# Four layers on one core: masks ahead, layer 0's mix in source order on VectorE and ScalarE, first norm row by row, a scaling halfway, statistics spread

## The chip, the cores and the metric

The kernel runs on one core of a Trainium2 chip, in one launch, with all data in F32. The metric is the device time in microseconds (us). The engines are TensorE (PE; its weight loads are listed apart as PEld), VectorE (DVE), ScalarE (ACT), GpSimd (POOL) and SyncE (SP), whose queue issues most of the DMAs. Each engine works through its own instructions one after the other.

## The reference

The input is 8 images of 56 × 56 positions with 192 channels. Four layers follow, each x + f(groupnorm(x)) with 32 groups:

```python
x = x + L0(_gn(x))   # p,q,v = silu(x@w+b); qv = q*v; out = (p*(toeplitz along w + toeplitz along h of qv)) @ o_w + o_b
x = x + L1(_gn(x))   # layer norm; rolled 7x7 windows, 6 heads, bias and mask added to the scores, softmax; projection
x = x + L2(_gn(x))   # 192 -> 384; 3x3 depthwise conv; mix of four exponential scans; layer norm; 384 -> 192
x = x + L3(_gn(x))   # 7x7 depthwise conv; layer norm; 192 -> 768, gelu, 768 -> 192; times gamma
return x
```

A group norm needs the mean and the variance of a whole image, so that each image's scale and shift come after its last element of the layer before. The layer norms are over the channels of one position.

## The kernel before, in words

**Stages.** The program goes layer by layer, each layer over all 8 images, with DRAM scratch between the steps. Image tiles have 128 partitions: 64 channels for the upper half of the image and the same 64 for the lower, by 3 channel groups j. Layer 0 has a first step (`layer0_qv`, L358, q and v of all images, written to the DRAM arrays left and right) and a second (`layer0_mix`, L463). Layer 1 takes four rows of windows per image. Layer 2 is `layer2_in` (L811), `layer2_mix` (L845, by channel groups over all images) and a loop over `layer2_out` (L968). Layer 3 begins with `layer3_in` (L983), which is interleaved with layer 2's output, then a depthwise convolution and the two large products.

**Order.** An instruction outside a `tc.manual_schedule(engines=...)` gets its place on its engine from a planner, which at compile time lists the instructions by the times it expects. Within such a block the engines named keep the order of the source; the others are still planned. Before the change layer 1's loop has PE in source order (L1279), the loop with layer 2's output and layer 3's input has VectorE (L1341), and the end of layer 3 has PE, ScalarE and VectorE (L1406). Layer 0 has none. `tc.keep_in_program_order` (in `layer2_in`) fixes single instructions. Tiles have a number of buffers (`bufs`, the pool's number where none is given): a write to a tile waits until the readers of the buffer's last use have ended, and a read waits for the write or the DMA.

**Masks.** `build_bias_mask` (L301) prepares attention bias plus mask for layer 1, in eight parts, during `layer0_qv` of images 1 on. `eighth(g)` (L324) clears the tile mk, which has one buffer, on GpSimd, loads two halves into it, adds six heads' bias on VectorE (L331) into bmt, one buffer as well, and stores bmt to DRAM (L334). q and v of the layer (L371 products, L377 bias addition on VectorE, L378 silu on ScalarE) run beside it.

**Mix.** For each image there are three passes g over channel chunks. A pass takes steps of 8 channels: `right_operand` copies part of a block's tile rt into rc (L409, on VectorE in even steps and ScalarE in odd ones, three buffers), `left_operand` copies lt into lc on GpSimd (two buffers), 8 or 16 small products go into one of two PSUM tiles op (L417), and the engine of that step copies op to o (L532). Operands are copied two steps ahead. A block's lt and rt are loaded by SyncE (L401), with two buffers each; pass 0 and 1 have four blocks of four steps, pass 2 one of eight. Between the steps of a pass, `between` runs the steps of the gate of the pass before (`layer0_gate`, L419): products pj (L429), silu on ScalarE (L434), transposes of o into ot, their product on VectorE (L443), products y (L450), and the addition to x on VectorE (L458). At the end of pass 0 the group norm's scaling xn of the image is written by three VectorE instructions, and the next image's x is loaded.

**First norm of layer 1.** `layer1_norm` (L622) is a generator. For each of four rows it writes xr on ScalarE (L636), the mean as a product (L644), subtracts on VectorE (L646), squares on ScalarE (L648), the variance as a product (L652) and copies it to rs (L653). After the fourth row it takes one square root (L654) and one reciprocal (L655) of all rows, and then for each row spreads rs by a product (L660) and multiplies (L662). For image 0 all of it is run before the first scores' Q, V and E parts (Q is L679); for the others, its steps are taken where `plan` (L1278) has an N.

**Layer 2's input.** `layer2_in` scales the image's x to xn in three VectorE instructions (L818), clears the padding on GpSimd (L821), then runs 15 tiles of products (L830, four PSUM tiles), each added to the bias on VectorE into pt (L838), and stores pt.

**Layer 2's output and layer 3's input.** For each image there are four groups k of rows and three j. Each (k, j) gives a product (L975) and the addition to x (L980). Pieces of the next image's layer norm statistics (`ln_pieces`, L190) come at i = 3k + j from 3 to 8; the steps of the image before's `layer3_in` are taken in between. `layer3_in` begins with 12 `bn_stats` (L144), two of its yields among them, goes on to the group sums (gh_m, L168), then the scaled image zp, its transposes zps (L1015) and the store.

Of the kernel before, what the change touches and what calls it, by code (L numbers as in the profile page):

```python
# [77 lines left out]
def kernel(ctx: ExitStack, tc: tile.TileContext, a: dict, out: bass.AP):  # L78
# [222 lines left out]
    def build_bias_mask(psum, pool, masks):  # L301
# [22 lines left out]
        def eighth(g):  # L324
            mk = pool.tile([128, 4, WN], F32, name="mk", bufs=1)
            nc.gpsimd.memset(mk, 0.0)
            for r in range(2):
                nc.gpsimd.dma_start(mk[64 * r:64 * r + WN], mask[g, r])
            bm = pool.tile([128, 3, 4, 2, WN], F32, name="bmt", bufs=1)
            for h in range(HEADS):  # L330
                nc.vector.tensor_tensor(  # L331
                    bm[:, h % 3, :, h // 3, :], mk, bt[:, h:h + 1, :].to_broadcast([128, 4, WN]), ALU.add
                )
            nc.gpsimd.dma_start(bmask[g], bm.rearrange("p a b c d -> p (a b c d)"))  # L334

        masks += [lambda g=g: eighth(g) for g in range(8)]
# [285 lines left out]
    def layer1_norm(b, x, pool, psum, consts):  # L622
# [7 lines left out]
        rs = pool.tile([128, TT], F32, name="rs1")  # L630
        yield xr
        sc, sh = scsh1[:, b, 0], scsh1[:, b, 1]
        for g in range(4):
# [19 lines left out]
            nc.vector.tensor_copy(rs[32 * g:32 * g + 32], vp)  # L653
        nc.scalar.activation(rs, rs, AF.Sqrt, bias=eps5)  # L654
        nc.vector.reciprocal(rs, rs)  # L655
        for g in range(4):
            yield
            gs = bass.ts(g, TT)
            bp = psum.tile([128, 512], F32, name="rstd", tag="mm", bufs=3)[:, 0:TT]
            nc.tensor.matmul(bp, sel[32 * g:32 * g + 32], rs[32 * g:32 * g + 32], start=True, stop=True)  # L660
            xs = xw[:, :, gs]
            nc.vector.tensor_tensor(xs, xs, bp.unsqueeze(1).to_broadcast([128, 3, TT]), ALU.mult)  # L662
# [148 lines left out]
    def layer2_in(b, x, pool, psum, w_in, b_in):  # L811
# [10 lines left out]
        nc.gpsimd.memset(xn[64:128, :, R2 - 3:R2, 0:W], 0.0)  # L822
        pt = pool.tile([128, C2, P2], F32, name="pt")
        nh = R2 // 2
        for i in range(nh):
# [12 lines left out]
            nc.vector.tensor_tensor(dst, ps[:, 0:ns, 0:C2], b_in[:, v, 0:ns], ALU.add)  # L838

# [128 lines left out]
    def layer2_out(k, j, y, x, psum, w_out):  # L968
# [11 lines left out]
        nc.vector.scalar_tensor_tensor(xs, ps[:, 0:nt], vec("b_out", j), xs, ALU.add, ALU.add)  # L980


    def layer3_in(b, x, zp, pool, psum):  # L983
# [3 lines left out]
        st = pool.tile([128, 3, NTH, 6], F32, name="gh_st")  # L987
        mv = pool.tile([128, 1, 3, 2], F32, name="gh_mv")
        for t in range(NTH):
            gn_piece(st, x, t)  # L990
            if t % 2:
                yield
# [228 lines left out]
    with ExitStack() as st:  # L1221
# [19 lines left out]
        layer0_mix(pool, blocks, psum, ops, w_p, w_o, loaded)  # L1241


    with ExitStack() as st:
# [23 lines left out]
        for _ in steps:  # L1268
            pass
# [256 lines left out]
```

## Time and profile before

| what | us |
|---|---|
| three runs of the kernel | 6127.55 median (6127.48 to 6136.09) |
| the profiled execution | 6119.55 |
| its span, with a mean granted PE clock of 0.943 | 6117.8 |
| PE busy | 5451.9 (89%) |
| VectorE busy | 3401.5 (56%) |
| ScalarE busy | 2216.8 (36%) |
| GpSimd busy | 1330.2 (22%) |

The span goes from the first instruction to the last in the profiled execution; the rest of its own time, 1.75 us, lies around it. The stages by that execution's clock: layer 0's first step 0 to 872, its mix 872 to 2103, layer 1 to 3440, layer 2's input to 3757, layer 2's mix to 4392, layer 2's output with layer 3's input to 4913, the convolution to 5252, and layer 3's products to 6118.

In a row of the timeline the first number is the start, the second the duration; then come engine, line and operation, out<-in by the program's names, and in brackets the idle time before it with what ended it. Rows of like instructions are put together with their number (x6).

### The profile page before, as it was taken

How to read it: one execution, taken by the hardware profiler on the slowest of the kernel's cores; microseconds unless marked ns; L12 is line 12 of the kernel's file. 1: busy time of each engine (PE TensorE's matmuls, PEld its weight loads, DVE VectorE, ACT ScalarE, POOL GpSimd, SP SyncE). 2: the span in 40 equal slices, each digit the busy share in tenths (PEclk: the TensorE clock that was granted, in tenths of full speed). 3: DMA queues.
4: the chain of work that ended last, by engine and by line, in shares of the span. 5: the costliest groups of instructions: out<-in, count | busy, mean ns of one | idle time of the engine just before them, and what ended most of it. 6: DMA issues, size and time to landing. Idle time of an engine off the chain costs nothing. (4 is left out here: it accounts for less than half of the span.)

```text
span 6117.8 us, 126576 instructions
## 1 busy us (share of the span) xinstructions
PE 5451.9 (89%) x55636; PEld 3509.4 (57%) x55636; DVE 3401.5 (56%) x4760; ACT 2216.8 (36%) x2938; POOL 1330.2 (22%) x867
## 2 busy tenths in 40 slices
PE   6799989999999888888888687999889889799999
PEld 5576766666666545555555455677544489444444
DVE  5677765565555445455454475888787601433331
ACT  2344444444444333333332101555466610333333
POOL 2100015444445212222222101433201100110100
PEclk8899999999999888999998898999989999899999
DMA  6799986666666614544533475667667588321210
GB/s 163 185 214 215 194 224 260 251 258 257 253 255 259 124 33 65 66 61 65 61 50 53 119 227 192 228 231 236 196 166 223 171 319 326 118 88 58 84 48 24
DMA packets 1034540, 1013.11 MB, mean 166 GB/s; under 512 B 826136, under 2 KB 958196, under 8 KB 1007220
## 3 DMA queue, kind: packets, MB, share of 16 engines
q1 hardware_dynamic: 1019424, 940.93, 54.5%
q0 software_dynamic: 8416, 39.40, 2.0%
q10 hardware_dynamic: 6148, 24.68, 1.3%
q8 instruction: 437, 7.16, 0.5%
q14 instruction: 115, 0.94, 0.0%
HBM read 676.28 MB, written 345.08 MB: 167 GB/s over the span
## 5 line engine op out<-in xcount | busy, mean ns | idle before, releaser
L371 PE MATMUL qv<-w_qv_sb,xn 64*112 64x288 f32 x5376 | 724.6, 426 | 51.1 <-DVE act L377 47.8
L409 POOL COPY lc<-lt 128x896 f32<-128x896 f32 (+1 forms) x320 | 572.7, 1806 | 620.4 <-PE op L417 602.6
L371 PEld LDWEIGHTS qv<-w_qv_sb,xn 64*112 64x112 f32 x5376 | 532.7, 184 | 238.1 <-DVE act L377 64.4
L378 ACT ACTIVATE act<-act 112x576 f32<-112x576 f32 x448 | 300.3, 682 | 462.1 <-DVE act L377 424.4
L1154 PE MATMUL ph<-y,w_sb 64*128 64x392 f32 x2304 | 398.4, 498 | 6.4 <-ACT hid L1158 6.4
L1165 PE MATMUL po<-hid,w_sb 128*64 128x392 f32 x2304 | 386.3, 494 | 0.0
L429 PE MATMUL pj<-xn,w_p_sb 64*128 64x392 f32 (+1 forms) x1920 | 373.4, 515 | 13.8 <-issue 10.5
L417 PEld LDWEIGHTS op<-rc,lc 128*56 128x56 f32 x9216 | 308.1, 136 | 127.1 <-issue 66.1
L417 PE MATMUL op<-rc,lc 128*56 128x56 f32 x9216 | 339.4, 221 | 43.9 <-POOL lc L409 25.7
L450 PE MATMUL y<-pp,w_o_sb 128*64 128x392 f32 (+1 forms) x1920 | 356.2, 504 | 21.9 <-DVE x L458 12.7
L377 DVE TENSOR_TENSOR act<-qv,b_qv 112x576 f32<-112x576 f32 x448 | 320.8, 751 | 90.8 <-PE qv L371 90.4
L1172 DVE TENSOR_TENSOR x<-x,z 128x392 f32<-128x392 f32 x96 | 71.0, 740 | 522.1 <-ACT z L1170 522.1
L409 ACT COPY rc<-rt 128x896 f32<-128x896 f32 (+1 forms) x160 | 256.8, 1605 | 238.7 <-PE op L417 219.8
L881 PE MATMUL cv<-zc,wt 128*128 128x224 f32 x1536 | 312.8, 355 | 24.2 <-DMA zc<-pd 24.2
L881 PEld LDWEIGHTS cv<-zc,wt 128*128 128x128 f32 x1536 | 290.2, 189 | 67.8 <-issue 51.9
L443 DVE TENSOR_TENSOR pp<-pp,ot 128x784 f32<-128x784 f32 (+1 forms) x160 | 154.6, 966 | 313.2 <-ACT pp L434 293.7
L1154 PEld LDWEIGHTS ph<-y,w_sb 64*128 64x128 f32 x2304 | 220.3, 188 | 176.3 <-issue 26.2
L729 POOL TENSOR_TENSOR e<-e,mx 128x1176 f32<-128x1176 f32 x64 | 139.8, 2184 | 812.5 <-DVE mx L728 629.6
L1055 PE MATMUL cps<-zc,wt 128*128 128x224 f32 x1536 | 299.1, 355 | 16.7 <-DMA zc<-zd 15.6
L830 PE MATMUL pin<-w_in_sb,xn 64*128 64x384 f32 x1392 | 251.5, 511 | 60.4 <-POOL xn L821 60.4
L1055 PEld LDWEIGHTS cps<-zc,wt 128*128 128x128 f32 x1536 | 289.0, 189 | 26.9 <-issue 19.4
L679 PE MATMUL qk_ps<-xr,wg 64*96 64x392 f32 x1536 | 299.5, 511 | 0.3 <-ACT oa L780 0.3
(211 smaller groups left out, 9113.6 us busy)
## 6 DMA issues: line engine op xcount, KB each, us to landing
lt<-left SPq DMA_DIRECT2D x72, 1792.0 KB
rt<-right SPq DMA_DIRECT2D x72, 1792.0 KB
left<-qv SPq DMA_DIRECT2D x224, 252.0 KB
right<-qv SPq DMA_DIRECT2D x448, 126.0 KB
wt<-in_band_dram SPq DMA_DIRECT2D x23, 2048.0 KB
wt<-in_band_dram SPq DMA_DIRECT2D x11, 4096.0 KB
zc<-pd SPq DMA_DIRECT2D x187, 232.0 KB
pd<-pt SPq DMA_DIRECT2D x7, 5568.0 KB
```

The lines of the kernel that those rows point to most:

```text
L371: nc.tensor.matmul(ps[s][:, which, 0:D1 // 2], xn[64 * s:64 * s + 64, j, bass.ts(i, 2 * W)], w_qv[64 * s:64 * s + 64, j, which, ns], start ...
L377: nc.vector.tensor_tensor(act, ps[s][:, :, 0:D1 // 2], b_qv[:, :, ns], ALU.add)
L378: nc.scalar.activation(act, act, AF.Silu)
L409: copy(c[:, 0:nu], raw.rearrange("p (w u d) -> p u d w", u=nu, d=64 // nu)[:, :, d0:d0 + 8])
L417: nc.tensor.matmul(op[64 * u:64 * u + W, i, :], lc[:, u, i], rc[:, u, i], start=True, stop=True)
L429: nc.tensor.matmul(ps[0:M, s, 0:TT], w_p[64 * s:64 * s + 64, j, d0:d0 + M], xn[64 * s:64 * s + 64, j, ts], start=(j == 0), stop=(j == 2),)
L450: nc.tensor.matmul(y[64 * s:64 * s + 64], w_o[0:M, c, 64 * j:64 * j + 64], pp[0:M, s], start=(c == gated[0][0]), stop=(c == gated[-1][0]),)
L679: nc.tensor.matmul(ps[s], wg[64 * s:64 * s + 64, j, c0:c0 + HC], xw[64 * s:64 * s + 64, j, gs], start=(j == 0), stop=(j == 2),)
L881: nc.tensor.matmul(dst, wt[:, c4 + i, 128 * q:128 * q + 128], zc[:, :, c4 + i, q:q + NPAIR], start=(q == 0), stop=(q == 1),)
L1055: nc.tensor.matmul(dst.rearrange("p (b n) -> p b n", n=NPAIR), wt[:, c4 + i, q * OP:(q + 1) * OP], zc[:, :, c4 + i, q:q + NPAIR], start=(q ...
L1154: nc.tensor.matmul(ps[:, s, 0:TT], w0[64 * s:64 * s + 64, j, m * 128:(m + 1) * 128], y[64 * s:64 * s + 64, j, ts], start=(j == 0), stop=(j ...
L1165: nc.tensor.matmul(ps[64 * s:64 * s + 64], w1[:, m, 64 * j:64 * j + 64], hid[:, m, s], start=(m == 0), stop=(m == 5),)
```

## The change

It has five parts. *Masks*: `eighth` is split into `load` and `add`, mk gets the pool's two buffers, mask 0 is loaded when the generator ends, and mask g + 1 is issued ahead of the addition of mask g. *Mix*: the call of `layer0_mix` stands in a `tc.manual_schedule` for VectorE and ScalarE. *First norm*: with `first=True` each row gets its own square root, reciprocal and multiplication; four steps (row 0 with its multiplication) run before the first scores, and the others one per part of the scores and then in the N steps. *Halfway*: the scaling of image b + 1 is a function of its own, `layer2_scale`, called after tile 7 of the 15 of image b (i = 7, so after eight tiles); image 0's is ahead of the loop. *Statistics*: each (k, j) of layer 2's output takes its own `bn_stats` right after the addition, `layer3_in` loses its 12 and two yields, the layer norm pieces are spread over i = 1 to 8 instead of 3 to 8, and the steps go one at a time up to i = 5 instead of 4.

```diff
@@ -321,19 +321,26 @@
             nc.vector.tensor_copy(bt[64 * r:64 * r + WN].rearrange("p h m -> p (h m)"), bp)
         mask = a["mask"].rearrange("(g q r) n m -> g r n q m", q=4, r=2)
 
-        def eighth(g):
-            mk = pool.tile([128, 4, WN], F32, name="mk", bufs=1)
+        mks = []
+
+        def load(g):
+            mk = pool.tile([128, 4, WN], F32, name="mk")
             nc.gpsimd.memset(mk, 0.0)
             for r in range(2):
                 nc.gpsimd.dma_start(mk[64 * r:64 * r + WN], mask[g, r])
+            mks.append(mk)
+
+        def add(g):
             bm = pool.tile([128, 3, 4, 2, WN], F32, name="bmt", bufs=1)
             for h in range(HEADS):
                 nc.vector.tensor_tensor(
-                    bm[:, h % 3, :, h // 3, :], mk, bt[:, h:h + 1, :].to_broadcast([128, 4, WN]), ALU.add
+                    bm[:, h % 3, :, h // 3, :], mks[g], bt[:, h:h + 1, :].to_broadcast([128, 4, WN]), ALU.add
                 )
             nc.gpsimd.dma_start(bmask[g], bm.rearrange("p a b c d -> p (a b c d)"))
 
-        masks += [lambda g=g: eighth(g) for g in range(8)]
+
+        load(0)
+        masks += [lambda g=g: (load(g + 1) if g < 7 else None, add(g)) for g in range(8)]
 
 
     def layer0_load(b, pool):
@@ -619,7 +626,8 @@
         rolled(x1[b], x, False, queues)
         return x
 
-    def layer1_norm(b, x, pool, psum, consts):
+    def layer1_norm(b, x, pool, psum, consts, first=False):
+
 
 
         ones2, ones32, sel = consts[4:]
@@ -628,6 +636,14 @@
         nc.gpsimd.memset(xr[:, 3 * NH:], 0.0)
         xw = xr[:, 0:3 * NH].rearrange("p (j n) -> p j n", j=3)
         rs = pool.tile([128, TT], F32, name="rs1")
+
+        def scaled(g):
+            gs = bass.ts(g, TT)
+            bp = psum.tile([128, 512], F32, name="rstd", tag="mm", bufs=3)[:, 0:TT]
+            nc.tensor.matmul(bp, sel[32 * g:32 * g + 32], rs[32 * g:32 * g + 32], start=True, stop=True)
+            xs = xw[:, :, gs]
+            nc.vector.tensor_tensor(xs, xs, bp.unsqueeze(1).to_broadcast([128, 3, TT]), ALU.mult)
+
         yield xr
         sc, sh = scsh1[:, b, 0], scsh1[:, b, 1]
         for g in range(4):
@@ -650,16 +666,22 @@
             vp = psum.tile([128, 512], F32, name="vps", tag="mm", bufs=3)[32 * g:32 * g + 32, 0:TT]
             for j in range(3):
                 nc.tensor.matmul(vp, ones32, sq[:, j], start=(j == 0), stop=(j == 2))
-            nc.vector.tensor_copy(rs[32 * g:32 * g + 32], vp)
+            if not first:
+                nc.vector.tensor_copy(rs[32 * g:32 * g + 32], vp)
+                continue
+            rg = rs[32 * g:32 * g + 32]
+            nc.scalar.activation(rg, vp, AF.Sqrt, bias=eps5[32 * g:32 * g + 32])
+            nc.vector.reciprocal(rg, rg)
+            yield
+            scaled(g)
+            yield
+        if first:
+            return
         nc.scalar.activation(rs, rs, AF.Sqrt, bias=eps5)
         nc.vector.reciprocal(rs, rs)
         for g in range(4):
             yield
-            gs = bass.ts(g, TT)
-            bp = psum.tile([128, 512], F32, name="rstd", tag="mm", bufs=3)[:, 0:TT]
-            nc.tensor.matmul(bp, sel[32 * g:32 * g + 32], rs[32 * g:32 * g + 32], start=True, stop=True)
-            xs = xw[:, :, gs]
-            nc.vector.tensor_tensor(xs, xs, bp.unsqueeze(1).to_broadcast([128, 3, TT]), ALU.mult)
+            scaled(g)
 
     def layer1_scores(g, xr, pool, psum, S, es, consts):
 
@@ -808,7 +830,7 @@
         queue.dma_start(x[64:128, :, 0:R2 - 3], src[:, :, R2 - 1:H])
         return x
 
-    def layer2_in(b, x, pool, psum, w_in, b_in):
+    def layer2_scale(b, x, pool):
 
         sc, sh = scsh2[:, b, 0], scsh2[:, b, 1]
         xn = pool.tile([128, 3, R2, 64], F32, name="xn2")
@@ -820,6 +842,10 @@
             ))
         nc.gpsimd.memset(xn[0:64, :, 0, 0:W], 0.0)
         nc.gpsimd.memset(xn[64:128, :, R2 - 3:R2, 0:W], 0.0)
+        return xn
+
+    def layer2_in(b, xn, pool, psum, w_in, b_in, halfway):
+
         pt = pool.tile([128, C2, P2], F32, name="pt")
         nh = R2 // 2
         for i in range(nh):
@@ -836,6 +862,8 @@
             dims = [list(z) for z in pt.ap]
             dst = bass.AP(pt.tensor, pt.offset + i, [dims[0], [nh, ns], [P2, C2]])
             nc.vector.tensor_tensor(dst, ps[:, 0:ns, 0:C2], b_in[:, v, 0:ns], ALU.add)
+            if i == nh // 2:
+                halfway()
 
         n = CG2 if b + 1 == nimg else 0
         if n:
@@ -965,7 +993,8 @@
                 bias=vec("be2", m), scale=vec("g2", m),
             )
 
-    def layer2_out(k, j, y, x, psum, w_out):
+    def layer2_out(k, j, y, x, st, psum, w_out):
+
 
         n0 = 4 * k
         nt = 2 * W * min(4, PH - n0)
@@ -978,18 +1007,14 @@
                 )
         xs = x[:, j, 2 * W * n0:2 * W * n0 + nt]
         nc.vector.scalar_tensor_tensor(xs, ps[:, 0:nt], vec("b_out", j), xs, ALU.add, ALU.add)
-
-
-    def layer3_in(b, x, zp, pool, psum):
+        nc.vector.bn_stats(st[:, j, k], xs)
+
+
+    def layer3_in(b, x, st, zp, pool, psum):
 
         sc = pool.tile([128, 1, 3], F32, name="sc3")
         sh = pool.tile([128, 1, 3], F32, name="sh3")
-        st = pool.tile([128, 3, NTH, 6], F32, name="gh_st")
         mv = pool.tile([128, 1, 3, 2], F32, name="gh_mv")
-        for t in range(NTH):
-            gn_piece(st, x, t)
-            if t % 2:
-                yield
         gn_aggregate(st, mv[:, 0])
         finish = gn_finish(mv, sc, sh, pool, psum, "gn")
         next(finish)
@@ -1238,7 +1263,8 @@
                 xpool.tile([128, 3, H // 2, W], F32, name="x1")
             x.append(layer1_load(0, xpool, (nc.sync, nc.gpsimd)))
 
-        layer0_mix(pool, blocks, psum, ops, w_p, w_o, loaded)
+        with tc.manual_schedule(engines={mybir.EngineType.DVE, mybir.EngineType.Activation}):
+            layer0_mix(pool, blocks, psum, ops, w_p, w_o, loaded)
 
 
     with ExitStack() as st:
@@ -1263,15 +1289,16 @@
 
         consts = (*consts, ones2, ones32, sel)
         xpool = x.pop(0)
-        steps = layer1_norm(0, x[0], pool, psum, consts)
-        xr = [next(steps)]
-        for _ in steps:
-            pass
+        own = layer1_norm(0, x[0], pool, psum, consts, True)
+        xr = [next(own)]
+        for _ in range(4):
+            next(own)
         if nimg > 1:
             x.append(layer1_load(1, xpool))
         values, (Q, V, E) = layer1_scores(0, xr[0], pool, psum, S, es, consts)
         for part in Q + [E[0], V[0], E[1], V[1]]:
             part()
+            next(own)
 
 
 
@@ -1300,6 +1327,7 @@
                     parts.update(zip("QVE", of_next))
                 for kind in plan:
                     if kind == "N":
+                        next(own, None)
                         next(steps, None)
                     elif parts.get(kind):
                         parts[kind].pop(0)()
@@ -1320,10 +1348,16 @@
         x = [layer2_image(0, xpool, nc.scalar)]
         w_in = resident("w_in", nc.scalar, pool)
         b_in = resident("b_in", nc.scalar, pool)
+        xn = [layer2_scale(0, x[0], pool)]
         for b in range(nimg):
             if b + 1 < nimg:
                 x.append(layer2_image(b + 1, xpool, nc.sync))
-            layer2_in(b, x[b], pool, psum, w_in, b_in)
+
+            def halfway():
+                if b + 1 < nimg:
+                    xn.append(layer2_scale(b + 1, x[b + 1], pool))
+
+            layer2_in(b, xn[b], pool, psum, w_in, b_in, halfway)
             if b == nimg - 3:
                 run(gn_finish(mv2[:, last], scsh2[:, last, 0], scsh2[:, last, 1], pool, psum, "pin"))
     with ExitStack() as st:
@@ -1372,13 +1406,15 @@
                         rows[0] = ln_rows(*var_next, eps5, pool)
                     following = scaled(*after, j)
                 if n >= 0:
-                    layer2_out(k, j, y, x[b], psum, w_out)
+                    if k == j == 0:
+                        gst = pool.tile([128, 3, 4, 6], F32, name="gh_st")
+                    layer2_out(k, j, y, x[b], gst, psum, w_out)
                     i = 3 * k + j
-                    if b + 1 < nimg and 3 <= i < 9:
-                        ln_pieces(st_next, ml[b + 1], range(NPAIR * (i - 3) // 6, NPAIR * (i - 2) // 6))
+                    if b + 1 < nimg and 1 <= i < 9:
+                        ln_pieces(st_next, ml[b + 1], range(NPAIR * (i - 1) // 8, NPAIR * i // 8))
                     if b + 1 < nimg and i == 8:
                         var_next = ln_var(in_halves(st_next), C2, pool)
-                    for _ in range(1 if i < 5 else 2):
+                    for _ in range(1 if i < 6 else 2):
                         next(steps, None)
                 if after and j < 2:
                     layer2_turned(after[1], j, following, y_next, psum)
@@ -1386,7 +1422,7 @@
             if k == 3:
                 run(steps)
                 nc.sync.dma_start(xd[b], x[b])
-                steps = layer3_in(b, x[b], zp, pool, psum)
+                steps = layer3_in(b, x[b], gst, zp, pool, psum)
         run(steps)
 
 
```

## The prediction

> **What bounds the kernel now.** The span is 6117.8 us, and TensorE is busy in 89% of it, so a part of the change is worth what it takes from TensorE's idle or cold time, or adds to it. I read the page's busy shares first, then windows over the five stretches that the change touches, then TensorE's list of waits, and last the tiles and timelines of the waits in question.
>
> Windows (start:end, length, then busy of PE, weight load, DVE, ACT, POOL, the granted clock, DMA share, GB/s):
>
> ```profile
> 225.00:310.00 85.00, 58.31 (x308) 42.55 (x308) 48.33 (x118) 18.63 (x28) 17.02 (x29) 0.76 0.66 162
> 874.00:2094.00 1220.00, 1144.51 (x15280) 755.44 (x15282) 696.80 (x906) 486.31 (x481) 574.83 (x325) 0.97 0.67 246
> 2103.00:2190.00 87.00, 53.15 (x546) 29.59 (x548) 33.13 (x37) 20.93 (x28) 12.73 (x14) 0.76 0.65 99
> 3469.00:3757.00 288.00, 255.73 (x1420) 148.77 (x1420) 201.71 (x148) 0.26 (x1) 14.63 (x34) 0.92 0.61 197
> 4395.00:4913.00 518.00, 434.53 (x2408) 223.11 (x2408) 362.86 (x688) 321.17 (x467) 58.85 (x78) 0.91 0.66 191
> ```
>
> In order they are the masks, layer 0's mix, the start of layer 1, layer 2's input product, and layer 2's output with layer 3's input. PE idles 26.7 us at the masks (85.00 − 58.31) at a clock of 0.76, about 75 us in the whole mix, and 32 us in layer 2's input. So there is much to win in short stretches, and little in the long one. What PE waited for:
>
> ```profile
> PE pin L830 <- POOL xn L821: 60.4, 8, 30.2
> PE tp L962 <- DVE yt L951: 57.9, 16, 16.9
> PE qv L371 <- DVE act L377: 47.8, 19, 6.0
> PE op L417 <- POOL lc L409: 25.7, 38, 1.9
> ```
>
> The first row is one start of 30.2 us and seven waits of (60.4 − 30.2)/7 = 4.3 us, one per image. About half of the third is the masks. The mask tile mk, and who waited for it:
>
> ```profile
>   DMA mk<-in_mask_dram: 34.6, 7
>   DVE bmt L331: 34.6, 7
> DMA to landing us min/median/max: 2.5/5.3/9.2
> ```
>
> VectorE stands 34.6 us before loads only just issued, and the bias additions of q and v (L377) are queued behind.
>
> **What the Trainium skill says.** "TensorE: Matmul & The Clock Gate", section "Part 1: The HAM clock gate", has PE fall to half clock after an idle window of a few us. The trace agrees: after a gap of 4.33 us the first tile of layer 2's input takes 3.70 us (start 3505.71, next eviction 3509.41) against 1.93 steady. The same page, "Architectural detail", says that ACT and DVE queues are strict FIFO: in the trace a Square stands ready at 2117.6 (VectorE's subtraction ends) and starts at 2126.58, behind activations that wait for a load. "ScalarE: Activation LUTs", "What ACT_TABLE_LOAD costs", gives 1283 ns; the trace shows 1.28 us at L654. "SBUF — State Buffer", "SBUF: two separate sides", says that VectorE and GpSimd share a port under a lock: a copy of rc (L409) takes VectorE 0.94 us alone and 2.15 beside GpSimd's copy of lc.
>
> **A, masks ahead.** A second mk buffer lets load g+1 start one image stretch before add g. The 34.6 us go. Late next is the bmt buffer, still single: the first addition waits for the store of the mask before, which lands 3.1 to 5.4 us after issue (median 4.2), with 0.8 to 2.2 us of other VectorE work between. About 3 us × 7 stay on VectorE, with the next L377 queued behind; PE's queued products hide 2 of each. PE keeps 7 × 1, and 4 of slow clock: −26 + 7 + 4 = **−15** (0, if the store is as late as the load was, to −26). GpSimd issues the same memset and DMAs, earlier.
>
> **B, mix in source order.** Nothing is added; the order of some 900 VectorE and 480 ScalarE instructions is fixed. The trace shows how far the present order is from it: 336 of 909 VectorE and 234 of 480 ScalarE instructions stand at their place in the source, most others within four places; what moves is that each rc copy comes one ahead of the gate's silu. Pass g = 1 (52.53 busy of 55 us) and g = 2 (47.00 of 47) are full of PE work, with two op buffers and three rc, so a silu or gate product in front of a copy costs about 0: what stands behind it on its engine, an rc or o copy, is needed two products later, and without that slack a pass would pay the 0.9 us of the silu per gate step. Pass g = 0 is different: its window shows DMA at 0.88, since a block's lt and rt take 4.7 us each and a block is used up in 9.5. ScalarE and SyncE there:
>
> ```profile
> 1505.36 0.53 ACT L532 COPY o<-op 120x448 f32<-120x448 f32 x1 [2.15 <-PE op L417]
> 1506.76 1.75 ACT L409 COPY rc<-rt 128x896 f32<-128x896 f32 x1 [0.87 <-PE op L417]
> 1508.84 0.91 ACT L434 ACTIVATE pp<-pj,vecs_sb 64x784 f32<-64x784 f32 x1 [0.33 <-PE pj L429]
> 1508.54 0.51 SPq L401 DMA_DIRECT2D rt<-right  x1
> ```
>
> The copy at 1506.76 is the last reader of its rt block; when it ends (1508.51) the next rt load goes out. In source order the silu is ahead of it, so the copy ends at 1508.84 + 0.91 + 1.75 = 11.5, 3.0 us later. If lt is loaded in that gap, most of it is covered; I take 0.65 us per block × 4 blocks × 8 images = +21, between 0 and 3.0 × 32 = 96. The three scalings to xn (5.2 us) now stand in one piece before the next rc and o: PE has 2 to 3 us to cover them, waits some 4 instead of 3: +8. The first pass and the last gate: +6 ± 6, with one gain against, since the wait of 10.5 us for x in the first pass (L429) falls to later, when x has long landed: −5. In all **+30** (−10 to +118).
>
> **C, first norm row by row.** Rows and PE at the start of layer 1:
>
> ```profile
> 2112.06 4.14 PE L644 MATMUL mean<-xr,ones 128*128 128x392 f32 x6
> 2127.84 4.10 PE L652 MATMUL vps<-sq,ones 128*32 128x392 f32 x6 [11.64 <-issue]
> 2162.45 5.89 PE L679 MATMUL qk_ps<-xr,wg 64*96 64x392 f32 x16
> ```
>
> Q starts 50 us after the first mean, when four rows are through. Row 0 alone from its vps at 2127.84: 2.2 products, 0.6 Sqrt and 1.28 table, 2.6 reciprocal, 1.7 rstd, 1.4 multiply: Q at about 2138, 24 us earlier, and up to 10 more if the Square isn't kept behind the waiting activations. Middle −28. Given back: rows 1 and 2 come between Q, E, V and the first softmax, 5 us of PE each, of which a softmax wait of 4.5 hides one: +5; row 3 in the N steps, with three more reciprocals of 2.6 on VectorE and table loads of 1.28, in front of copies that PE waits for: +5. **−18** (−3 to −30).
>
> **D, scaling halfway.** The turn of an image:
>
> ```profile
> 3501.42 0.84 DVE L838 TENSOR_TENSOR pt<-pin,b_in_sb 128x384 f32<-128x384 f32 x1 [0.39 <-PE pin L830]
> 3502.11 3.26 DVE L818 TENSOR_SCALAR xn<-x,scsh 128x1680 f32<-128x1680 f32 x3
> 3509.41 1.54 DVE L838 TENSOR_TENSOR pt<-pin,b_in_sb 128x768 f32<-128x768 f32 x1 [4.05 <-issue]
> ```
>
> The scaling is between two images with PE empty. Moved to tile 8 of 15, it has 15 × 1.93 = 29.0 us of products to hide in; VectorE's load per image is 14 × 1.54 + 0.84 + 3.3 = 25.7, and four PSUM tiles (7.7 us) carry PE over it. What is late next is x: its load takes 11.5 us and lands 6 us before halfway; with the store of pt (12 us) DMA has 23.5 of 29 us. New stage: 31.6 + 7 × 29.0 + 4.5 (the aggregate after image 5) = 239 against 287: **−48** (−30 to −52). Without the cover each image pays 3.3 us again, −25.
>
> **E, statistics spread.**
>
> ```profile
> 4879.23 5.70 DVE L144 BATCH_NORM_STATS2 gh_st<-x2o 128x6 f32<-128x392 f32 x12
> 4885.16 3.15 PE L168 MATMUL gh_m<-gh_mv,gmath_sb 128*128 128x1 f32 x14 [6.34 <-DVE gh_mv L148]
> ```
>
> The last image's 12 statistics stand bare before gh_m (6.34 us, and 3.15 cold against 1.72): −7. In the seven others they go from one place on VectorE to twelve, of equal sum; PE idles 6.5 us per period of 58.4, of which I take 1 each: −7. Against it, the first pieces at i = 1 want the next ml some 1 to 5 us before it lands (VectorE in order, so x2o waits behind): +4. **−10** (−25 to +10).
>
> **Sum.** −15 + 30 − 18 − 48 − 10 = −61. The profiled execution took 6119.55 us (span 6117.8 and 1.75 around it), so 6058.5; it lies 8 us under the median of 6127.55, and from that 6066.5 comes. I say **6065**.
>
> **Rivals.** (1) *Slower: the rt load behind the silu.* If the 3.0 us delay of L401 are all exposed, the 32 blocks of pass g = 0 cost 96 and B 96 + 22 (scalings 12, first pass 6, finish 4) = +118; with −91 for the rest, **6154**. It decides from (91 − 22)/32 = 2.2 us per block. For it: DMA runs at 0.88 there and the load is on its path. Against: lt is free to go first, and GpSimd already waits 0.64 for it. (2) *Source order is free*, B = 0: −91, **6036**. For it: PE idles only 75 us in the mix. (3) *New waits take the place of the old*: the bmt store gives A = 0, the row's Square stays behind the loads so that C = −5, D = −40, E = 0, B = +30: −15, **6112**. For it: single bmt buffer, load just in time. (4) *The planner's order differs so little that nothing shows*, within 0.2% (12 us, about what a measurement can tell): against it D, a plain removal.
>
> **Chances.** Forecast 0.37, rival 2 0.22, rival 3 0.14 (on the faster side), no change 0.05, rival 1 0.22: faster 0.73, same 0.05, slower 0.22. The low end is −91 with bounds of −30 more: 6005; the high end cuts through rival 1 at 6150.
>
> **What would show it.** mk's wait on VectorE from 34.6 to under 5, and one for the store instead; "pin <- POOL xn" from 60.4 to about 30; Q from 2162 (counted from the mix's end) 18 to 34 us earlier; gh_m's 6.34 under 2; the mix at 1250 instead of 1220, with rt issues of pass g = 0 at 10.2 instead of 9.5 apart. I am wrong if the mix grows by over 90, or layer 2's input doesn't fall under 250.

## The result and the profile after

The changed kernel takes 6107.52 us (median of 12 runs, 6095.21 to 6125.61), the kernel before 6128.76 (12 runs, 6110.45 to 6143.45): a ratio of 0.9967, with a 95% interval of 0.9954 to 0.9979. It is some 20 us faster, where 63 were forecast (6127.55 less 6065). The profiled execution took 6100.29 us, span 6098.5, 19.3 under the span before.

To see where the 19.3 us come from I took the start of the same products in both traces (the first of a stage or of an image) and subtracted:

| stretch | before | after | difference | forecast |
|---|---|---|---|---|
| start to the end of q and v (masks) | 869.4 | 850.8 | −18.6 | −15 |
| to the last y of the mix | 1232.4 | 1248.0 | +15.7 | +30 |
| to the first projection of layer 1's image 1 (first norm) | 290.2 | 279.8 | −10.5 | −18 |
| rest of layer 1, to the start of layer 2's input | 1077.8 | 1077.6 | −0.1 | 0 |
| layer 2's input (halfway) | 286.9 | 242.8 | −44.2 | −48 |
| layer 2's mix (not changed) | 633.2 | 637.5 | +4.3 | 0 |
| layer 2's output, layer 3's input (statistics) | 532.2 | 564.3 | **+32.1** | **−10** |
| rest | 1195.7 | 1197.7 | +2.0 | 0 |

The windows over the five stretches of the changed kernel, in the order and with the columns of the prediction's:

```profile
225.00:310.00 85.00, 67.10 (x438) 45.36 (x438) 59.20 (x137) 24.50 (x37) 15.24 (x26) 0.89 0.80 192
855.40:2091.10 1235.70, 1153.09 (x15286) 770.36 (x15287) 639.10 (x907) 471.42 (x481) 582.38 (x325) 0.97 0.65 243
2100.10:2187.10 87.00, 63.12 (x687) 35.05 (x689) 39.13 (x40) 31.21 (x43) 14.91 (x15) 0.74 0.64 97
3455.40:3699.60 244.20, 241.88 (x1420) 170.09 (x1420) 196.79 (x148) 0.27 (x1) 14.96 (x35) 0.97 0.72 232
4341.60:4891.70 550.10, 462.31 (x2408) 232.25 (x2408) 370.18 (x688) 321.94 (x467) 54.09 (x78) 0.88 0.62 180
```

Layer 2's input is now full: PE idles 2.3 of 244.2 us. In the last stretch the same 2408 products take 462 us of PE instead of 435, at a clock of 0.88 instead of 0.91. Most of the loss is here. PE's list of waits for the whole changed kernel:

```profile
PE tp L990 <- DVE yt L979: 65.6, 27, 18.5
PE op L424 <- DVE o L539: 32.2, 9, 16.3
PE pin L856 <- POOL xn L843: 30.1, 1, 30.1
```

The seven waits of 4.3 us of pin are gone and its start is left; the mix has got nine waits for o, of which one is of 16.3 us. VectorE's masks (waits of bmt):

```profile
DVE bmt L336 <- DMA bmask<-bmt: 16.9, 6, 5.0
```

As forecast, the load's 34.6 us are replaced by a shorter wait for the store of the mask before. The turn of an image in layer 2's input, on VectorE:

```profile
3486.93 0.86 DVE L864 TENSOR_TENSOR pt<-pin,b_in_sb 128x384 f32<-128x384 f32 x1 [0.39 <-PE pin L856]
3488.94 1.55 DVE L864 TENSOR_TENSOR pt<-pin,b_in_sb 128x768 f32<-128x768 f32 x1 [1.15 <-PE pin L856]
```

The next image's first eviction starts 2.0 us after the last of this one instead of 8.0, and no scaling stands between. PE at the start of layer 1:

```profile
2109.11 4.29 PE L660 MATMUL mean<-xr,ones 128*128 128x392 f32 x6
...
2132.76 7.34 PE L701 MATMUL qk_ps<-xr,wg 64*96 64x392 f32 x24 [1.47 <-DVE xr L645]
```

Q starts 23.7 us after the first mean instead of 50.4. And the tail, on VectorE:

```profile
4863.73 0.39 DVE L1010 BATCH_NORM_STATS2 gh_st<-x2o 128x6 f32<-128x224 f32 x1
```

This is the last statistic, and the only one after the last addition, where a block of 5.70 us stood. gh_m now waits 1.15 us instead of 6.34:

```profile
4864.34 2.21 PE L168 MATMUL gh_m<-gh_mv,gmath_sb 128*128 128x1 f32 x14 [1.15 <-DVE gh_mv L148]
```

**Where the last stretch loses.** Of its 32.1 us, 10.9 are in image 0, 25.3 in images 1 to 7, 1.5 at the start, and the tail gives back 5.6. In image 0 VectorE waits (timeline of the changed kernel):

```profile
4381.86 2.36 DVE L190 BATCH_NORM_STATS2 ln_st<-ml 112x6 f32<-112x384 f32 x3 [9.67 <-DMA ml<-md]
```

The pieces at i = 1 ask for the ml of image 1 before it has landed. In VectorE's list of waits for the whole stretch this is the only one for an ml of a later image, so during images 1 to 7 VectorE never waits for ml:

```profile
DVE ln_st L190 <- DMA ml<-md: 9.7, 1, 9.7
```

For images 1 to 7 the two windows, before and then after:

```profile
4477.10:4878.80 401.70, 364.81 (x2096) 186.69 (x2095) 289.21 (x540) 274.16 (x399) 45.93 (x62) 0.96 0.65 190
```

```profile
4436.20:4863.20 427.00, 390.38 (x2096) 194.82 (x2095) 295.44 (x540) 274.61 (x399) 41.25 (x62) 0.94 0.61 180
```

PE's idle time is the same (36.9 and 36.6 us): the 25 us are in PE's busy time, for the same 2096 products. So neither a wait on VectorE nor one on a DMA explains them. I worked out two things from PE's records in these windows: the part of the busy time lost to a slow clock (each piece of busy time times one minus the clock granted in it), and the number of runs, that is how often PE passes from products of one tile (po, tp, zps, gh) to another's.

### The profile page after: what moved, and what is told of

It is laid out like the page before. It is cut to its first block, busy times and chain, and to the rows that moved or that the text cites. A ratio compares the mean times of both kernels' runs of the same rounds, so it can differ in the third digit from the quotient of the medians.

```text
span 6098.5 us, 126582 instructions
## 1 busy us (share of the span) xinstructions
PE 5483.8 (90%) x55636; PEld 3545.8 (58%) x55636; DVE 3355.5 (55%) x4759; ACT 2209.4 (36%) x2945; POOL 1330.5 (22%) x867
## 5 line engine op out<-in xcount | busy, mean ns | idle before, releaser
L378 PEld LDWEIGHTS qv<-w_qv_sb,xn 64*112 64x112 f32 x5376 | 514.9, 183 | 235.2 <-DVE act L384 51.4
L424 PE MATMUL op<-rc,lc 128*56 128x56 f32 x9216 | 345.3, 221 | 75.7 <-POOL lc L416 36.0
L384 DVE TENSOR_TENSOR act<-qv,b_qv 112x576 f32<-112x576 f32 x448 | 321.0, 752 | 83.5 <-PE qv L378 83.2
L457 PE MATMUL y<-pp,w_o_sb 128*64 128x392 f32 (+1 forms) x1920 | 354.7, 503 | 2.4 <-DVE pp L450 2.3
L441 ACT ACTIVATE pp<-pj,vecs_sb 128x784 f32<-128x784 f32 (+1 forms) x160 | 146.3, 914 | 498.8 <-PE pj L436 487.3
L1080 PEld LDWEIGHTS cps<-zc,wt 128*128 128x128 f32 x1536 | 290.1, 189 | 27.3 <-issue 19.6
```

The lines of the kernel that those rows point to most:

```text
L378: nc.tensor.matmul(ps[s][:, which, 0:D1 // 2], xn[64 * s:64 * s + 64, j, bass.ts(i, 2 * W)], w_qv[64 * s:64 * s + 64, j, which, ns], start ...
L384: nc.vector.tensor_tensor(act, ps[s][:, :, 0:D1 // 2], b_qv[:, :, ns], ALU.add)
L424: nc.tensor.matmul(op[64 * u:64 * u + W, i, :], lc[:, u, i], rc[:, u, i], start=True, stop=True)
L457: nc.tensor.matmul(y[64 * s:64 * s + 64], w_o[0:M, c, 64 * j:64 * j + 64], pp[0:M, s], start=(c == gated[0][0]), stop=(c == gated[-1][0]),)
L1080: nc.tensor.matmul(dst.rearrange("p (b n) -> p b n", n=NPAIR), wt[:, c4 + i, q * OP:(q + 1) * OP], zc[:, :, c4 + i, q:q + NPAIR], start=(q ...
```

## The experiments

**Which part.** The parts alone and left out:

```
stats_alone:    before + statistics
all_but_stats:  before + masks + mix + first norm + halfway
mix_alone:      before + the manual_schedule around layer0_mix
three_parts:    before + masks + first norm + halfway
```

Each part is its hunks of the diff above, word for word; the edit of mix_alone, which all_but_stats has and three_parts has not, is

```diff
-        layer0_mix(pool, blocks, psum, ops, w_p, w_o, loaded)
+        with tc.manual_schedule(engines={mybir.EngineType.DVE, mybir.EngineType.Activation}):
+            layer0_mix(pool, blocks, psum, ops, w_p, w_o, loaded)
```

> The kernel before with part E (statistics spread) alone. Theory: E is the part that failed. In the changed kernel's profile the stage from the first output product to the last is 36 us longer than before: 10 us in the first image, where VectorE waits 9.7 us for the load of the next image's ml, 14 to 16 us of PE clock at half more often, and about 10 us because the planner splits the output products into more runs on PE (158 against 138). 7 us come back in the tail. So E alone makes the kernel 25 to 35 us slower, ratio 1.004 to 1.006. Rival, the prediction's own step: E alone saves 10 us, ratio 0.998, and the loss in that stage came from the state in which the other parts leave it.

> The changed kernel without part E, so masks, mix, first norm and halfway. Theory: without E the kernel keeps what the others gain: -18 masks, +16 mix, -11 first norm, -44 halfway, that is -57, ratio 0.991, and the last stage takes 518 us again. Rival: the last stage is longer whatever E does, and the ratio stays at 0.996 to 0.997.

> The kernel before with part B (mix in source order on VectorE and ScalarE) alone. Theory from the two profiles: +16 us, ratio 1.0025, nearly half of it in the first image, and pass 0 is not longer. Rival, the prediction's step: +30 us, ratio 1.005, in pass 0, whose rt loads go out 3 us later per block; second rival: 0, and the +16 of the profiles is a difference of clock.

> The kernel before with masks, first norm and halfway scaling, without the mix's source order and without the spread statistics. Theory: the gains add up, -18 -11 -44 = -73 us, ratio 0.988. Rival: part of the first norm's gain hangs on the order in the mix, or some is given back later, ratio 0.991 or more.

| run | us | ratio (95%) | mix | last stretch |
|---|---|---|---|---|
| stats_alone | 6152.15 | 1.0065 (1.0052 to 1.0079) | 1229.2 | 566.6 |
| all_but_stats | 6063.54 | 0.9916 (0.9901 to 0.9930) | 1242.5 | 534.1 |
| mix_alone | 6133.04 | 1.0037 (1.0024 to 1.0050) | 1236.3 | 534.2 |
| three_parts | 6045.62 | 0.9891 (0.9874 to 0.9907) | 1218.5 | 532.8 |

(Here and below the mix is timed from its first product op to its last y: 1225.1 before, 1240.7 after.) The statistics are a loss by themselves, 34 us in their own stretch, and without them the stretch is back. The mix in source order is a loss too. The three others gain 71 us of medians together (6116.3 to 6045.6 on that chip), and their three stretches in the table above 73, so the gains simply add.

**Which half of the statistics, and which engine of the mix.** The two stretches don't touch, so each kernel tests one thing in each. All have masks, first norm and halfway.

dve_order_ln_spread (VectorE's order, layer norm pieces):

```diff
+        with tc.manual_schedule(engines={mybir.EngineType.DVE}):
...
-                    if b + 1 < nimg and 3 <= i < 9:
+                    if b + 1 < nimg and 1 <= i < 9:
```

act_order_gn_spread (ScalarE's order, group norm statistics with the pace of the steps):

```diff
+        with tc.manual_schedule(engines={mybir.EngineType.Activation}):
...
+        nc.vector.bn_stats(st[:, j, k], xs)
```

o_first_pe_order (all five parts, o ahead of rc, PE's order in the last stretch):

```diff
-                    right_operand()
                     layer0_products(ops[n % 2], nu, lcs[n], rcs[n])
-                    left_operand()
...
                     copies[n % 2](o[0:part, :, at:at + 8], ops[n % 2][0:part].rearrange("p d h -> p h d"))
+                    right_operand()
+                    left_operand()
...
-        st.enter_context(tc.manual_schedule(engines={mybir.EngineType.DVE}))
+        st.enter_context(tc.manual_schedule(engines={mybir.EngineType.DVE, mybir.EngineType.PE}))
```

> Masks, first norm and halfway as in the changed kernel; the mix in source order on VectorE alone; of part E only the layer norm pieces over i = 1 to 8, the group norm statistics as before. Two stages are read, each against 1218 to 1229 us (mix, planned) and 532 to 534 us (end of layer 2's mix to the convolution, part E not done). Theory for the mix: an rc copy that waits for its rt load stands on VectorE in front of the copy of op to o and of the gate's work; VectorE alone in source order gives most of the loss, 1230 to 1240. Rival: it is ScalarE's order (the silu ahead of the rc copy), then 1218 to 1229 here. Theory for part E: the spread pieces cost the late ml of the first image, 10 us, and little else: 542 to 548. Rival: the pieces cause all of the loss, 563 or more.

> As the run before, with the mix in source order on ScalarE alone, and of part E only the group norm statistics per (k, j), the layer norm pieces as before. Theory: the mix 1220 to 1230; the stage of part E: no late ml, the tail 6 us shorter, but the planner's more divided PE order and the slower clock after the one-column group products stay, 550 to 558. Rivals: ScalarE's order costs the mix 10 or more; the statistics alone gain 6, 527.

> All five parts, with two edits. In the mix, still in source order on both engines, the copy of op to o is written ahead of the rc copy for two steps later. Theory: nothing then waits behind a late rt load but the gate, and the mix comes back to 1218 to 1229. Rival: the order of copies is not the cause, 1236 or more. In part E's stage PE is kept in source order as VectorE is, so that no product group is split by another tile. Theory: the splits are worth about 10 us, and the stage falls from 564 to 567 to about 555, with the wait for ml and part of the slow clock left. Rival: PE in source order waits more for yt than it saves, 567 or more.

Last stretch: 584.8, 543.3 and 602.5 us. Mix: 1222.7, 1250.0 and 1306.3 us. (Each is from one profile. The last stretch without part E came out within 2 us in four profiles, 532.2 to 534.2; the planned mix between 1218 and 1236 in seven.) Each of the six lies outside what my theory gave for it, and in five the rival's range came true. The layer norm pieces alone cost 52 us, not 10. Both halves together cost less (564) than these alone. PE in source order is far worse. And in the mix it is ScalarE's order that costs, about 23 us over the planned builds' middle of 1227 (and more than both orders together, 1236 to 1243), while VectorE's costs nothing in sum: with it pass 1 takes 61.4 us per image instead of 59.6, and pass 0 39.0 instead of 41.5 (images 1 to 7). With o ahead of rc the loss becomes 79.

What the pieces alone do is seen in a later image. VectorE, then PE, in dve_order_ln_spread:

```profile
4672.86 2.41 DVE L190 BATCH_NORM_STATS2 ln_st<-ml 112x6 f32<-112x384 f32 x3 [3.41 <-DMA ml<-md]
4675.17 2.90 DVE L144 BATCH_NORM_STATS2 gh_st<-x2o 128x6 f32<-128x392 f32 x6
4677.98 0.68 DVE L1008 SCALAR_TENSOR_TENSOR x2o<-po,vecs_sb,x2o 128x448 f32<-128x448 f32 x1
```

```profile
4671.24 3.22 PE L1003 MATMUL po<-y,w_out_sb 128*64 128x448 f32 x14
4678.72 1.75 PE L1003 MATMUL po<-y,w_out_sb 128*64 128x448 f32 x2 [4.26 <-DVE x2o L1008]
```

ml lands 25 us after its issue at 4647.84, which is 3.4 us too late for i = 1. The pieces, six group norm statistics and only then the addition that frees PE's PSUM tile follow each other on VectorE; PE idles 4.26 us and comes back at half clock (1.75 us for two products; two take 0.97 at 4724.86 of the changed kernel, below). Over images 1 to 7 the clock was at half for 96 us in this kernel, against 32 before.

**One slot later, and the first image apart.**

In ln_from_two (group norm statistics as before) and in both_from_two (both halves) the condition of the pieces is the first of these lines, in first_image_late (both halves) the second; the ranges follow.

```diff
+                    if b + 1 < nimg and 2 <= i < 9:
...
+                    if b + 1 < nimg and (1 if b else 3) <= i < 9:
```

> Masks, first norm and halfway; the mix planned; group norm statistics as before; layer norm pieces over i = 2 to 8, 7 slots, against 1 to 8 in the run dve_order_ln_spread (585 us) and 3 to 8 before (533). Theory: at i = 1 the pieces ask for ml some 3 us before it lands, VectorE waits with the output's addition queued behind, PE idles past 3 us and its clock is halved; a slot later ml is there and the stage takes 533 to 545. Rival: it is the pieces' place in general, and the stage stays over 560.

> Masks, first norm, halfway and the whole of part E, but the layer norm pieces during image 0 over i = 3 to 8 as before, for the other images over 1 to 8. Theory: the wait for the first ml falls (9.7 us in the changed kernel); image 0's period goes from 76.8 to about 70, where the run with the group norm statistics alone has it at 72.1, and the other seven stay at 427. Rival: image 0's period stays at 75 or more, so that it is not the wait.

> Masks, first norm, halfway and part E with the layer norm pieces over i = 2 to 8 for all images. Theory: images 1 to 7 lose their time to PE's order, not to ml, so they come near the run with the group norm statistics alone (411.7 us) only as far as PE's runs and slow clock do; 410 to 422 against 427, in step with the number of runs (about 0.3 us each beyond 315). Rival: at i = 1 the pieces cost something whatever PE's order, and at i = 2 the seven images take 405 or less.

Each ran once, as did the three kernels before them. The columns from "PE busy" on are for images 1 to 7.

| last stretch: kernel | whole | image 0 | images 1 to 7 | PE busy there | lost to slow clock | busy without it | runs |
|---|---|---|---|---|---|---|---|
| before | 532.2 | 65.9 | 401.7 | 364.8 | 15.1 | 349.7 | 315 |
| ln_from_two | 543.8 | 73.8 | 404.8 | 373.2 | 18.7 | 354.5 | 320 |
| act_order_gn_spread | 543.3 | 72.1 | 411.7 | 374.3 | 19.6 | 354.7 | 336 |
| both_from_two | 547.5 | 73.8 | 415.0 | 377.3 | 13.9 | 363.4 | 359 |
| first_image_late | 562.6 | 72.7 | 430.6 | 393.2 | 33.1 | 360.0 | 362 |
| after | 564.3 | 76.8 | 427.0 | 390.4 | 26.6 | 363.8 | 368 |
| stats_alone | 566.6 | 75.7 | 431.8 | 395.0 | 31.6 | 363.4 | 368 |
| dve_order_ln_spread | 584.8 | 73.0 | 445.6 | 399.0 | 45.0 | 354.0 | 319 |
| o_first_pe_order | 602.5 | 83.5 | 458.5 | 366.9 | 54.8 | 312.1 | 195 |

A slot later the pieces alone fall from 585 to 544: the late ml is the cause there, as expected. In images 1 to 7 of ln_from_two VectorE waits for no ml any more. With both halves the same slot takes 17 us from the stretch, 12.7 of them slow clock (26.6 to 13.9), and none of the 14 us that the busy time without slow clock grew by. The images 1 to 7 take 415.0 us, as expected (410 to 422). It can't be a wait for ml that went here, since images 1 to 7 of the changed kernel have none. What went are three falls of PE's clock behind the products gh_v, each of 6.8 us at half, which is 10 us lost; the last section shows one of them.

The 14 us go with the runs: 315 runs and 350 us, 359 to 368 runs and 360 to 364, 195 runs and 312; about 0.3 us for each. (Two kernels at 319 and 320 runs lie 5 us above that line.) Rows of the changed kernel's timeline show what a run costs. A po group left whole is one row, and split by a transpose it is two:

```profile
4715.61 2.48 PE L1004 MATMUL po<-y,w_out_sb 128*64 128x448 f32 x12
4718.01 0.99 PE L1040 MATMUL zps<-ident,zp 128*128 128x128 f32 x7
...
4719.93 0.97 PE L1004 MATMUL po<-y,w_out_sb 128*64 128x448 f32 x4
4720.83 0.41 PE L990 MATMUL tp<-ident,yt 112*128 112x112 f32 x2
4721.17 1.72 PE L1004 MATMUL po<-y,w_out_sb 128*64 128x448 f32 x8
4722.83 1.09 PE L1040 MATMUL zps<-ident,zp 128*128 128x128 f32 x8
...
4724.86 0.97 PE L1004 MATMUL po<-y,w_out_sb 128*64 128x448 f32 x2
```

From its start to the next tile the whole group takes 2.40 us, the split one 2.90. Some 0.2 us of the difference are the two tp products themselves, so two more runs cost 0.3 us, or 0.15 each. By this estimate the 53 more runs of the changed kernel are 8 of the 14 us.

The runs miss a second thing. po products mostly start in pairs, about 0.01 us apart, and the next pair follows 0.37 us later (448 columns); a product that starts alone, with no other within 0.06 us, takes the same 0.37 us. So the four products at 4719.93 take 0.97 us, and the two at 4724.86 take 0.97 as well. By PE's records, of the 1008 po products of images 1 to 7, 144 start alone before and 192 in the changed kernel; it is 168 and 164 in the two kernels above the line, and none in o_first_pe_order. 48 more alone are 24 more starts of 0.37 us, 9 us at most. For the two kernels above the line both terms together give 5.0 and 4.5 us, about what was measured; for the changed kernel they give 17 where 14 were measured, and for act_order_gn_spread, with 208 alone, 15 where 5 were. So the kind and the size are right, but it isn't an exact account.

PE is not in source order here; with other VectorE instructions between, the planner put zps, gh and tp between po's products more often (158 runs of po instead of 138). PE in source order has the fewest runs and yet loses, since it then idles 92 us instead of 37 and is at half clock for 119.

In image 0 the wait for ml falls with first_image_late, and takes 4 of the 10.9 us with it. The other 7 stay, and act_order_gn_spread, which has no such wait in image 0, shows 6 of them, so they come with the group norm half. The pieces alone lengthen image 0 by the wait itself, and at i = 2 it is still there: VectorE waits 7.8 us for that ml in ln_from_two and 3.9 in both_from_two.

**The mix: the rt load, and the best version.**

last_image_stats (masks, first norm, halfway, and statistics per (k, j) in the last image; the others as before):

```diff
+                        gst = pool.tile([128, 3, 4, 6], F32, name="gh_st") if b + 1 == nimg else None
```

rc_ahead_of_gate (the same, and the mix in source order with rc a gate step earlier):

```diff
-                    right_operand()
                     layer0_products(ops[n % 2], nu, lcs[n], rcs[n])
...
                     n += 1
+                    right_operand()
                     between()
```

> Masks, first norm and halfway, the mix planned as before, and of part E only the statistics per (k, j) of the last image; all other images as before. Theory: the tail's saving of 5 to 6 us is kept without the cost in the other images, so the stage goes from 533 to 527 or 528 and the ratio from 0.9891 to 0.988. Rival: the saving of the tail comes with the planner's more divided order there, 533 or more.

> As the run before, but with the mix in source order on VectorE and ScalarE, and in the source each rc copy is written one gate step earlier, after the copy of op to o and ahead of the silu. Theory: the loss of the mix in source order comes from ScalarE, where the last rc copy of a block stands behind a silu and lets the next rt load go 3 us later; with the copy ahead, the rt load of the block goes out at 3 us from the block's start as when planned (5.8 in source order), and the mix takes 1225 us or less against 1236 to 1242 in source order and 1218 to 1229 planned. Rival: the late rt load is hidden and the loss is from source order as such, 1236 or more.

last_image_stats: 6039.03 us, ratio 0.9875 (0.9859 to 0.9890), last stretch 525.8. This is as expected, and the lowest ratio of the study, though its interval overlaps that of three_parts (last stretch 532.8): the tail's saving is had without the cost. rc_ahead_of_gate: 6070.95 us, 0.9931 (0.9918 to 0.9943), mix 1251.1. SyncE in pass 0 of image 4, first in mix_alone (the block starts at 1478.9), then in rc_ahead_of_gate (1484.2):

```profile
1484.75 0.51 SPq L401 DMA_DIRECT2D rt<-right  x1
1486.51 0.51 SPq L401 DMA_DIRECT2D lt<-left  x1
```

```profile
1487.02 0.51 SPq L408 DMA_DIRECT2D rt<-right  x1
1491.76 0.51 SPq L408 DMA_DIRECT2D lt<-left  x1
```

The rt load goes out 5.8 us after the start in source order and 2.8 with rc ahead, as in the planned kernel (2.9). So the delay of 3 us is real, and it is not the cost: with it gone pass 0 takes 38.8 us on average instead of 41.2 (images 1 to 7, against mix_alone), pass 1 64.0 instead of 60.9, and the mix is longer. What comes in its place is another copy that waits for a load. ScalarE in pass 1 of rc_ahead_of_gate, then PE:

```profile
1556.32 1.74 ACT L416 COPY rc<-rt 128x896 f32<-128x896 f32 x1 [6.81 <-DMA rt<-right]
1557.95 0.54 ACT L539 COPY o<-op 120x448 f32<-120x448 f32 x1
```

```profile
1558.63 0.50 PE L424 MATMUL op<-rc,lc 128*56 128x56 f32 x5 [3.93 <-ACT o L539]
```

The copy of o, whose products have long ended, stands behind an rc copy whose rt hasn't landed, and PE has no free op. In source order one of the two copies always stands first; put o first, and rc comes late instead.

## Why the prediction was wrong, point by point

- **A, masks:** right. The wait for the load is gone, the wait for the store has come (16.9 us in six, forecast 3 × 7). The stretch is 18.6 us shorter, and 12 between the means of the eleven profiles with the part and the three without (forecast 15).
- **B, mix:** forecast +30, measured +15.7 in the two profiles and +12.6 over builds (mean of three, 1239.8, against 1227.2 of seven planned ones). Most of it is not by the mechanism of the forecast. That had +21 from rt loads in pass 0; they do go out 3.0 us later, to the tenth, and pass 0 is no longer for it, since the lt load now follows its rt load within 1.8 us and both land in time. The +8 of the scalings did come: PE waits for xn 7.6 us in six, before 0.4 in one. For the rest, some 5 us are in image 0: PE now stands 16.3 us before the second block is there, where the planned kernel stood 10.5 and then did products pj under that load. Some 2 us per image are in pass 1, where PE idles 0.7 us longer (an o copy waits behind an rc copy) and is busy longer, with 42 runs instead of 35; passes 0 and 2 are 0.5 and 0.8 us shorter. Rival 1 hung on the rt loads too, and falls with them.
- **C, first norm:** right in kind, 10.5 for 18 (13.1 between the means over the same builds). Q came 26.7 us earlier, close to the middle of the forecast (28), though the Square of row 0 still stood behind activations that wait for a load of x; rows 1 to 3 gave back 16 instead of 10.
- **D, halfway:** right, 44.2 for 48.
- **E, statistics: this step failed.** It said −10 and was +32; that is 42 us, as much as lies between forecast (−61) and measurement (−19.3) in the profiles; what the other rows are off cancels. The tail's saving was as worked out (5.6 for 7). The term that failed is the −7 for the seven other images (statistics "of equal sum; PE idles 6.5 us per period of 58.4, of which I take 1 each"). They took 25 us more instead. These 25 us are in PE's busy time, which the forecast took as fixed. The same work at other places on VectorE made the planner place PE's work differently: some 14 us of the 25 are more runs (368 instead of 315) and more po products that start alone (192 instead of 144), and 11 are slow clock, of which 10 are the three falls behind gh_v. The second term is "+4" for the late ml: its wait is 9.7 us in image 0, not 1 to 5, and there is none in images 1 to 7; it cost some 4, so the two errors about cancel. (With the pieces alone it does come in five of those seven images, 0.3 to 3.4 us each, and the slow clock takes 30 us more than before.) The third is image 0: some 7 us that aren't the ml, for which the forecast had nothing.
- **Rival 3** has the nearest number, 6112, but by luck: it had 0 for the masks, 5 for the first norm and 0 for the statistics, where −18.6, −10.5 and +32.1 were measured.
- What stays open: that runs and products alone are the cause of the 14 us is a relation over nine kernels and an estimate from single rows, not an edit of PE's order alone (the one that did this changed the waits as well); and of image 0's other 7 us I know only that the group norm half brings them.

## What to carry to other kernels

Where one engine is placed by a planner, moving equal work on another engine is not free: count how often the bound engine changes between products, before and after, and look at its busy time for the same number of instructions, not only at its waits. A piece of work that needs a load belongs where the load has landed with a margin, since the engine that waits holds back what stands behind it. A short stop of PE can cost a second time in clock, and so, by the next section, may very small products that follow each other closely. And where several edits go in together, take each one alone: here two of five were losses of 34 and 13 us in their stretches, under the gains of the other three.

## What had not been expected of the hardware

PE's clock also falls while PE is busy. Windows of 2.5 us of the changed kernel, where gh_m and gh_v (14 products of one column each) follow each other closely:

```profile
4688.20:4690.70 2.50, 2.50 (x20) 1.65 (x19) 1.47 (x6) 0.72 (x1) 0.00 (x0) 1.00 0.53 188
4690.70:4693.20 2.50, 2.50 (x13) 1.99 (x13) 2.46 (x5) 0.67 (x2) 0.00 (x0) 0.63 1.04 436
4693.20:4695.70 2.50, 2.50 (x10) 1.41 (x8) 1.55 (x4) 2.10 (x3) 0.75 (x1) 0.50 1.10 470
```

PE has no gap, and the clock is at half for 6.8 us. In the same place before, 1.72 us of po lay between gh_m and gh_v, and the clock held:

```profile
4727.38 1.72 PE L168 MATMUL gh_m<-gh_mv,gmath_sb 128*128 128x1 f32 x14 [0.19 <-DVE gh_mv L148]
4729.03 1.72 PE L975 MATMUL po<-y,w_out_sb 128*64 128x448 f32 x8
4730.68 1.72 PE L168 MATMUL gh_v<-gh_d,gmath_sb 128*128 128x1 f32 x14
```

It is not a single case. In the changed kernel it happens in images 5, 6 and 7, each time 1.1 us after the first gh_v. In images 1 to 7 of the eleven kernels in which PE doesn't stop between these products, there are 17 times when 1.2 to 1.3 us lie between the end of gh_m and the first gh_v, and in 13 of them the clock fell 0.7 to 1.6 us after that (the three here, five each in stats_alone and first_image_late). In the other 60, with 1.6 us or more between, it never fell in that place.

The Trainium skill, "TensorE: Matmul & The Clock Gate", section "Part 1: The HAM clock gate", ties the half clock to an idle window of about 3.4 us. Of the nine stretches at half in images 1 to 7 of this trace, which are 3.4 or 6.8 us long, six come with stops of PE of 1.7 to 3.2 us, shorter than that window, and three with none that the records show. So here shorter stops and busy stretches bring the half clock too, and the measurement decides. That the one-column products bring the three is argued from their place in these profiles; no edit moved them alone.
